# LayerNorm statistics of every ninth group on ScalarE, one conv chunk of two bands back on VectorE, and weights loaded and prepared later, in a fused attention and feed-forward block

## The chip, the cores and the metric

The kernel runs on one core of a Trainium2 chip. The metric is the device time of one execution in microseconds (us). The engines are named as in the profile: PE is TensorE's matmuls and PEld its weight loads, DVE is VectorE, ACT is ScalarE, POOL is GpSimd, and SP is the engine that here only issues transfers.

## The reference, cut to what matters

The input is 16 images of 128 channels by 96 x 96 pixels in float32. Each image goes through one transformer block:

```
xn1 = layernorm(x over channels)                    # per pixel, 9216 pixels per image
q, k, v = xn1 @ wq.T, xn1 @ wk.T, xn1 @ wv.T        # 8 heads of 16 channels
q, k = l2norm over the pixels                       # attention between channels
attn = softmax(q k^T / sqrt(16))                    # 16 x 16 per head
x = x + (attn v) @ wp.T
xn2 = layernorm(x over channels)
h1 = w_in @ xn2                                     # 1x1, 128 -> 512 channels
h2 = depthwise 3x3 convolution of h1                # one 3x3 filter per channel
x = x + w_out @ gelu(h2)                            # 1x1, 512 -> 128
```

The LayerNorm needs, for each pixel, the mean and the variance over the 128 channels and the power -1/2 of the variance.

## The kernel before, in words

**Tiling.** Channels lie on the 128 partitions. An image has 8 bands of 12 rows (1152 pixels), 24 units of 4 rows (384 pixels) and, for the LayerNorms, 18 groups of 4 x 128 pixels. The 512 hidden channels are 4 chunks of 128.

**One LayerNorm group** (`pixels`; suffix a for the first norm, b for the second). PE transposes four 128 x 128 tiles into one PSUM bank `pT` (`forth`, L609), so that pixels lie on partitions. DVE takes mean and sum of squared deviations with `bn_stats`, two tiles per instruction (`stats`, L616), into `st`. POOL makes the variance (`variance`, L623) and its power (`power`, L627) into `rstd`. For norm b DVE makes the shift `nb` (L631). ACT writes the scaled tiles to `zT` (`scaled`, L663 for a, L667 for b). For norm a PE adds each tile to a Gram matrix (`gram`, L677), from which the attention follows as small matrices per image. PE transposes back (`back`, L714), and ACT copies to the padded tile `xn` (`place`, L718, L720, L724). There are two `pT` banks for both norms. In image 0 the groups of norm a and the first five of norm b use the four `h` banks, and DVE scales half of each (L650, L654). The attention's result is one matrix per image, applied by `mix` (L566), with the residual added by ACT and a transfer (L575, L578), or by DVE in image 0 (L572).

**Feed-forward, by band and chunk** (`conv_job`). PE makes the hidden chunk (`hidden`, L899) and ACT copies it to `h1` (`kept`, L904, and the two halo rows, L895). Of the nine taps of the depthwise filter, ACT multiplies two or three (`product`, L912), and POOL-issued transfers add them up (`add_products`, L921). DVE does the remaining six or five with one fused multiply-add over 1152 pixels each (`tap`, L917). ACT applies GELU (L925). The fourth chunk is done in some bands by PE alone (`by_matmuls`, L967): nine matmuls per unit, with the 1x1 and the tap multiplied together beforehand in `comp`, and GELU straight from PSUM (L973). Which bands these are is said by `by_pe`:

```python
def by_pe(g):
    k = NG - 1 - g
    return k in PE_LAST if k < NB else k % PE_OF in PE_BANDS
```

`ffn_out` (L990) multiplies the four chunks by `w_out`, DVE adds the result to `x` (L997), and SP stores the band (L1001).

**The order.** Every piece of work is an `op` of a class `Plan`, with an engine, a place, an estimated cost and the tiles that it reads and writes. `Plan.order()` runs a list scheduler over them at build time: an engine takes its ready operation of the lowest place. A place is the position in the sequence of conv jobs plus an offset per kind from the table `AT`. So each engine has a fixed list of instructions, which it works off in order, and waits stand where the list and the data put them. The times in `Plan` are estimates for ordering only.

**The start.** SP loads the bands of `x` (L546). ACT issues the loads of the small vectors, of `wv` and of the depthwise weights `dw` (L276, L283, L288), and, after its third `place` copy, five loads of the other weights (L420 to L424). DVE first prepares `unit` and `ratio` from `dw` (L487 to L493) and the shift vectors (L478 to L482), and only then takes its first `bn_stats`.

Of the kernel before, what the change touches and what calls it, by code (L numbers as in the profile page):

```python
# [9 lines left out]
F32 = mybir.dt.float32  # L10
AF = mybir.ActivationFunctionType
ALU = mybir.AluOpType
# [5 lines left out]
UR = 4  # L18
BR = 12
PE_CHUNK = 3  # L20
PE_BANDS = (0,)
PE_OF = 2
PE_LAST = (0, 1, 2, 4, 5, 7)
TINY = 1e-20
UNIT_MIN = 1e-18
# [5 lines left out]
X1_BUFS, XB_BUFS, PR_BUFS, H3_BUFS, ZT_BUFS = 2, 6, 5, 10, 3  # L31
IN_TURN = ("tr", "h3", "pr", "xb", "x1")
AT = dict(
    load_w=20.7, weights=-42.35, zeros=-138.3, load_a=-151.9, forth_a=0.1, stats_a=-36.15, variance_a=263.5,
    power_a=249.55, scaled_a=74.15, gram=2.55, back_a=-28.75, place_a=112.3, attention=-146.85, mix=-33.95,
    residual=283.8, mixed=-159.7, add_x=-437.65, forth_b=0.35, stats_b=-221.75, variance_b=76.3, power_b=-236.6,
    shift_b=-162.65, scaled_b=19.7, back_b=1.45, place_b=-30.7,
    halo=161.95, hidden=3.15, kept=-18.75, products=83.25, add_last=-139.85, tap=10.15,
    add_first=-120.05, gelu=196.55, conv=2.95, conv_gelu=9.4, out=6.5, add=-10, store=164.8, mix_0=-40.75,
    residual_0=378.9, mixed_0=-198.6, add_x_0=-364.75, gram_0=9.85, forth_a_0=-6.55, forth_b_0=2.65,  # L40
    stats_a_0=-99.05, stats_b_0=-205.9, scaled_a_0=-81.4, scaled_b_0=247.4, back_a_0=-172.15, back_b_0=-50.5,
    place_a_0=-98.9, place_b_0=-35, shift_b_0=-201.25, late=-145.5,
)
STEP = dict(scaled=0.3, hidden=0.1, products=0.5, tap=0.166, conv=1.6, conv_tap=0.03, out=0.8, out_part=0.05)
SLACK = 300
NORM1_END = 6.0
EARLY = 5
WAIT = dict(POOL=350, SP=1300, ACT=1300)
T_WEIGHTS = 12000
T_VARIANCE = 420  # L50
T_POWER = 1000
T_ADD, T_MOVE = 3060, 1640
# [2 lines left out]
class Plan:  # L55
# [14 lines left out]
    def op(self, engine, ns, place, work, reads, writes, result, own=None, dma=0, two=False):  # L70

        k = len(self.ops)
        needs = {}
        for t in reads:
            if t in self.writer:
                needs[self.writer[t]] = True  # L80
        for t in writes:
            if t in self.writer:
                needs[self.writer[t]] = True
            for r in self.readers.get(t, ()):
                needs[r] = True
# [12 lines left out]
        self.ops.append((engine, ns, place, work, list(needs), new, result, own or result, dma, two))  # L98
# [111 lines left out]
def tile_restormer_block(  # L210
# [76 lines left out]
    per_unit = const.tile([P, NCH], F32, name="per_unit")  # L287
    nc.scalar.dma_start(out=dw, in_=w_dw.rearrange("(n p) o kh kw -> p n (o kh kw)", p=P))  # L288

    wvb = const.tile([P, 1], F32, name="wvb")  # L290
    ccol = const.tile([P, 2, 2], F32, name="ccol")
    ncq = const.tile([1, P], F32, name="ncq")
    none = const.tile([P, 1], F32, name="none")
# [56 lines left out]
    def at(kind, place, i=1):  # L350
        return place + AT[kind if i else kind + "_0"]
# [25 lines left out]
    def dve(ns, p, f, r, w, two=False):  # L377
        op("DVE", ns, p, f, r, w, ns + 120 + SLACK, ns + 120, two=two)
# [1 line left out]
    def add(p, f, r, w):  # L380
        op("POOL", 950, p, f, r, w, 1400 + SLACK, dma=T_ADD)

    def move(p, f, r, w, ns):
        op("SP", 60, p, f, r, w, 900 + SLACK, dma=ns)

    def act(ns, p, f, r, w):
        op("ACT", ns, p, f, r, w, ns + 150 + SLACK, ns + 150)
# [20 lines left out]
    def weights(p):  # L408
# [4 lines left out]
        def loads():  # L413
            a, b = (h3p.tile([P, BR * W], F32, tag="h3", name=f"weights_{k}") for k in range(2))
            v["win"] = a[:, :HID].rearrange("p (n c) -> p n c", c=P)
            v["wout"], v["wp"] = a[:, HID : 2 * HID], a[:, 2 * HID : 2 * HID + P]
            v["wqk"], v["wqkT"] = b[:, : 2 * P], b[:, 2 * P : 4 * P]
            v["wt"] = b[:, 4 * P : 8 * P].rearrange("p (t c) -> p t c", c=P)
            v["centre"], v["w1centre"], v["wvT"] = b[:, 8 * P : 9 * P], b[:, :P], b[:, P : 2 * P]
            nc.scalar.dma_start(out=v["wqk"][:, :P], in_=wq)  # L420
            nc.scalar.dma_start(out=v["wqk"][:, P:], in_=wk)
            nc.scalar.dma_start(out=v["wp"], in_=wp)
            nc.scalar.dma_start(out=v["win"], in_=w_in.rearrange("(n p) c kh kw -> p n (c kh kw)", p=P))
            nc.scalar.dma_start(out=v["wout"], in_=w_out.rearrange("c j kh kw -> c (j kh kw)"))  # L424

        def transposed(kind, parts, kept, gives):

# [68 lines left out]
            for n in range(NCH):  # L496
                nc.vector.tensor_scalar(v["wt"][:, n, :], v["win"][:, n, :], unit[:, n : n + 1], None, ALU.mult)

        op("ACT", 400, at("load_w", p), loads, [], mine, T_WEIGHTS, dma=2 * T_MOVE)
        dve(1400, at("weights", p), units, [], [("w", "in")])  # L500
        dve(400, at("weights", p), shifts, [], [("w", "in"), ("w", "conv"), ("w", "shift")])
        transposed(
            "weights", lambda: [v["wqk"][:, :P], v["wqk"][:, P:], v["wp"], wv_sb], keep_qkp, ["qk"]
        )
# [35 lines left out]
    def load(p, i, b):  # L540
        key = x_key(i, b, False)

        def go():
            pool, of = (xpool, xbs) if key == "xb" else (x1pool, x1s)
            of[i, b] = pool.tile([P, BR * W], F32, tag="x", name=f"x_{i}_{b}")
            nc.sync.dma_start(out=of[i, b], in_=x_band(i, b))  # L546

        move(p, go, [], [(key, (i, b), s) for s in range(UPB)], T_MOVE)

    def norm(i, second, place_of):  # L550

# [40 lines left out]
        def pixels(s, m):  # L592
# [18 lines left out]
            def stats(j):  # L611
# [5 lines left out]
                    d["st"][:, j, :], d["pT", qs[h]][:, k : k + 2, :].rearrange("p t c -> p c t")  # L617
                )

            def variance():  # L620
                d["mv"] = d["st"].rearrange("p j (t v) -> p (j t) v", v=3)
# [6 lines left out]

            def shift():
                nb = d["nb"] = small.tile([P, QB * QT], F32, tag="nb", name=f"nb_{name}_{m}")  # L630
                nc.vector.scalar_tensor_tensor(nb, d["mv"][:, :, 1], -1.0, d["rstd"], ALU.mult, ALU.mult)  # L631

            def zT(q):
                if q in zTs:
# [71 lines left out]
        def channels(s, u):  # L706

            d = {}

            def back():  # L710
                d["pB"] = p_bk.tile([P, UT], F32, tag="bk", name=f"pB_{name}_{u}")
                for j in range(TPU):
                    q, k = divmod(u * TPU + j, QT)
                    nc.tensor.transpose(d["pB"][:, j * P : (j + 1) * P], zTs[q][:, k, :P], ident)  # L714

            def place():
                if second:
                    nc.scalar.activation(interior(i, u), rows(d["pB"]), AF.Identity, bias=b2)  # L718
                else:
                    nc.scalar.copy(interior(i, u), rows(d["pB"]))  # L720

            def place_row(k, r, row):
                to = window(xns[k], r, 1, 1)
                nc.scalar.activation(to, rows(d["pB"])[:, row : row + 1, :], AF.Identity, bias=b2)  # L724

            copies = []
            if second and u % UPP == 0 and u > 0:
                copies.append((part_of(i, u * UR - 1)[0], PART + 1, 0, UPP))
            if second and u % UPP == UPP - 1 and u < NU - 1:
# [5 lines left out]
            act(t_act(UT, 1) - 43 if second else t_copy(UT), at("place" + ab, s, i), place, [pb, ("w", "shift")], [z_unit(i, u)])  # L735
# [340 lines left out]
```

## Time and profile before

| what | value |
|---|---|
| median of 3 runs | 4175.92 us (4175.73 to 4176.47) |
| the profiled execution | 4175.62 us |
| its span in the profile | 4173.9 us |
| busy: PE, PEld, DVE, ACT, POOL | 4142.5, 2679.6, 4070.0, 3693.7, 2479.5 us |
| transfers | 827.64 MB, mean 198 GB/s |

The profile covers one execution from its first to its last instruction, the span. The execution took 1.7 us more than that. A group of instructions is given by line, engine and operation, with the tile written, the tiles read, the count, the busy time, the mean duration of one, and the idle time of the engine just before. Successive instructions of one engine overlap, so the distance from start to start is less than a duration. Where a mean is used as a cost, this matters.

### The profile page before, as it was taken

What the parts mean: (1) busy time and instruction counts of PE and PEld (TensorE: products, weight loads), DVE (VectorE), ACT (ScalarE), POOL (GpSimd) and SP (SyncE); (2) the same over time, 40 slices, a digit from 0 to 9 for tenths busy, and PEclk for the clock granted to TensorE, in tenths of its full rate; (3) what the DMA queues carried; (4) which work ended last, traced back from release to release, by engine and by line L of the source; (5) the groups of instructions that cost most, each with busy time, mean ns of one, the idle gap of its engine ahead of it and who ended that gap; (6) DMA issues with size and microseconds to landing.
All of it is one profiled execution on the core that took longest, in us unless ns stands there. A gap on an engine that the chain in (4) does not pass through costs nothing.

```text
span 4173.9 us, 52446 instructions
## 1 busy us (share of the span) xinstructions
PE 4142.5 (99%) x17457; PEld 2679.6 (64%) x17457; DVE 4070.0 (98%) x4676; ACT 3693.7 (88%) x6970; POOL 2479.5 (59%) x2391
## 2 busy tenths in 40 slices
PE   8999999999999999999999999999999999999999
PEld 7666666666666666666666666666666666666565
DVE  6999999999999999999999999999999999999998
ACT  5899989899899989989898898998998999899885
POOL 4656566565665656656576565666756567565442
PEclk9999999999999999999999999999999999999999
DMA  2999999999999999999999998999999999998997
GB/s 88 197 188 215 194 208 208 203 208 197 205 208 201 204 198 212 200 205 211 193 202 205 199 215 185 211 200 209 208 198 202 201 209 201 203 204 184 201 193 159
DMA packets 203935, 827.64 MB, mean 198 GB/s; under 512 B 23568, under 2 KB 24976, under 8 KB 203664
## 3 DMA queue, kind: packets, MB, share of 16 engines
q0 software_dynamic: 164160, 672.47, 83.0%
q1 hardware_dynamic: 37152, 151.01, 9.9%
q8 instruction: 138, 2.26, 0.2%
q10 hardware_dynamic: 2352, 0.81, 0.1%
q14 instruction: 133, 1.09, 0.1%
HBM read 148.26 MB, written 75.50 MB: 54 GB/s over the span
## 4 chain that ended last, share of the span: by engine, by line
PE 88%; DVE 4%; DMA 3%; ACT 3%; POOL 1%; issue 1%; ACTq 0%; POOLq 0%; DVEq 0%
PE h L967 25%; PE h L990 21%; PE h L899 19%; PE g L677 5%; PE h L566 5%; DVE h L917 3%; PE pB_b L714 3%; PE pT_b L609 3%; PE pB_a L714 3%; PE pT_a L609 2%; DMA h<-pr 2%; DMA pr<-pr 1%; ACT pr L912 1%; ACT h L904 0%; DVE st_a L616 0%
## 5 line engine op out<-in xcount | busy, mean ns | idle before, releaser
L917 DVE SCALAR_TENSOR_TENSOR h<-h,ratio,h 128x1152 f32<-128x1152 f32 x2104 | 2915.2, 1407 | 3.6
L912 ACT ACTIVATE pr<-h,ratio 128x1152 f32<-128x1152 f32 x1018 | 1301.6, 1290 | 65.1 <-DMA h<-pr 37.6
L967 PE MATMUL h<-xn,comp 128*128 128x384 f32 x3564 | 1269.3, 485 | 0.0
L990 PE MATMUL h<-h,woutT 128*128 128x384 f32 x3072 | 1137.1, 486 | 1.0 <-ACT h L904 0.4
L899 PE MATMUL h<-xn,winT 128*128 128x384 f32 (+1 forms) x2676 | 1078.6, 500 | 1.1 <-ACT h L904 1.0
L967 PEld LDWEIGHTS h<-xn,comp 128*128 128x128 f32 x3564 | 647.9, 189 | 394.9 <-issue 12.6
L921 POOL DMA_DIRECT2D pr<-pr x573 | 562.6, 989 | 493.2 <-ACT pr L912 385.7
L904 ACT COPY h<-h 128x384 f32<-128x384 f32 (+1 forms) x1338 | 667.9, 520 | 182.0 <-PE h L899 162.1
L990 PEld LDWEIGHTS h<-h,woutT 128*128 128x128 f32 x3072 | 554.2, 190 | 327.2 <-issue 10.3
L921 POOL DMA_DIRECT2D h<-pr x445 | 424.7, 956 | 531.5 <-DVE h L917 119.0
L899 PEld LDWEIGHTS h<-xn,winT 128*128 128x128 f32 x2676 | 475.5, 190 | 269.2 <-issue 39.2
L917 DVE SCALAR_TENSOR_TENSOR h<-h,ratio 128x1152 f32<-128x1152 f32 x446 | 627.3, 1411 | 13.5 <-ACT h L904 5.3
L925 ACT ACTIVATE h<-h 128x1152 f32<-128x1152 f32 x448 | 536.0, 1198 | 17.0 <-DMA h<-pr 13.9
L627 POOL TENSOR_TENSOR rstd_a<-ve_a,mhalf 128x4 f32<-128x4 f32 x288 | 534.4, 1856 | 12.7
L627 POOL TENSOR_TENSOR rstd_b<-ve_b,mhalf 128x4 f32<-128x4 f32 x288 | 506.8, 1760 | 11.3
L667 ACT ACTIVATE zT<-pT_b,nb_b,rstd_b 128x128 f32<-128x128 f32 x1132 | 430.5, 478 | 24.3 <-DVE nb_b L631 21.3
L623 POOL TENSOR_SCALAR ve_b<-st_b 128x4 f32<-128x4 f32 x288 | 293.8, 1020 | 219.8 <-DVE st_b L616 204.8
L623 POOL TENSOR_SCALAR ve_a<-st_a 128x4 f32<-128x4 f32 x288 | 276.8, 961 | 226.0 <-DVE st_a L616 211.8
L663 ACT ACTIVATE zT<-pT_a,rstd_a 128x128 f32<-128x128 f32 x1080 | 316.6, 406 | 19.8 <-POOL rstd_a L627 19.4
L677 PEld LDWEIGHTS g<-zT 128*128 128x128 f32 x2304 | 297.2, 191 | 56.9 <-issue 3.8
L677 PE MATMUL g<-zT 128*128 128x129 f32 x2304 | 305.2, 275 | 0.0
L566 PE MATMUL h<-xn,mwT 128*128 128x384 f32 x768 | 284.3, 490 | 5.6 <-ACT h L904 2.7
(173 smaller groups left out, 3578.6 us busy)
## 6 DMA issues: line engine op xcount, KB each, us to landing
pr<-pr POOLq DMA_DIRECT2D x573, 576.0 KB, 7.3
h<-pr POOLq DMA_DIRECT2D x445, 576.0 KB, 6.9
x<-in_x_dram SPq DMA_DIRECT2D x128, 576.0 KB, 6.2
out_dram<-x SPq DMA_DIRECT2D x127, 576.0 KB, 5.2
x<-in_x_dram POOLq DMA_DIRECT2D x122, 576.0 KB, 6.9
out_dram<-x SPq DMA_DIRECT2D x3, 192.0 KB, 1.9
weights<-in_L_conv_w_in_dram ACTq DMA_DIRECT2D x1, 256.0 KB, 2.9
weights<-in_L_conv_w_out_dram ACTq DMA_DIRECT2D x1, 256.0 KB, 3.0
```

What stands on the lines that cost most here:

```text
L566: nc.tensor.matmul(rows(pm), lhsT=mats[i][0], rhs=interior(i, u), start=True, stop=True)
L623: nc.gpsimd.tensor_scalar(ve, d["mv"][:, :, 2], 1.0 / C, EPS, ALU.mult, ALU.add)
L627: nc.gpsimd.tensor_tensor(rstd, d["ve"], mhalf, ALU.pow)
L677: nc.tensor.matmul(grams[i][:, : P + 1], lhsT=zt[:, :P], rhs=zt, start=(q == 0 and k == 0), stop=(q == NU * TPU // QT - 1 and k == QT - 1),)
L899: nc.tensor.matmul(rows(ph), lhsT=winT[:, n, :], rhs=window(xn, r0 + r, e - r, 1), start=True, stop=True)
L904: nc.scalar.copy(window(h1_, r, e - r, 1), rows(d.pop(("ph", r))))
L912: nc.scalar.activation(to, shifted(t), AF.Copy, scale=ratio[:, n, t : t + 1])
L917: nc.vector.scalar_tensor_tensor(h3, shifted(t), ratio[:, n, t : t + 1], onto, ALU.mult, ALU.add)
L921: nc.gpsimd.dma_start(out=to, in_=d["pr", t], accum_op=ALU.add)
L925: nc.scalar.activation(h3, h3, AF.Gelu)
L967: nc.tensor.matmul(d["pc"], lhsT=comp[:, t, :], rhs=window(xn, r0 + dy, UR, dx), start=(t == 0), stop=(t == 8),)
L990: nc.tensor.matmul(rows(d["po"]), lhsT=woutT[:, n, :], rhs=h3s[g, n][:, s * UR : (s + 1) * UR, :], start=(k == 0), stop=(k == NCH - 1),)
```

## The change

1. In every image one norm group in nine (group numbers 1 and 10 of norm a, 4 and 13 of norm b, not those that use the `h` banks) takes its statistics on ACT. For each of its four tiles one pass with `Identity` and scale -1/128 accumulates minus the mean, and one pass with `Square` and that value as bias accumulates the sum of squared deviations. The elementwise results go to a tile `junk` that nobody reads. The two `bn_stats` of the group on DVE are left out, and the sign in `shift` is turned.
2. `PE_BANDS` and `PE_OF` say 15 of 31 bands in place of 1 of 2. Counted over the 128 bands with the last 8 as they were, PE does the fourth chunk in 64 bands in place of 66, and DVE, ACT and the transfers in 64 in place of 62.
3. The five weight loads move from ACT's queue to SP's, behind the eight band loads of image 0. The preparation of `unit`, `ratio` and the shift vectors is ordered behind these loads, and in DVE's list it stands after the statistics of the twelfth group. ACT gets one small copy at its start, so that its table is loaded there.
4. The table `AT` has other values throughout, so all five lists are ordered anew.

```diff
-PE_BANDS = (0,)
-PE_OF = 2
+PE_BANDS = (0, 2, 4, 6, 8, 10, 12, 14, 16, 18, 20, 22, 24, 26, 28)
+PE_OF = 31
...
+BY_ACT_OF, BY_ACT_A, BY_ACT_B = 9, (1,), (4,)
+T_SQUARES = 840
...
-T_WEIGHTS = 12000
+T_START = 2300
...
+    none = const.tile([P, 1], F32, name="none")
+    nc.scalar.copy(none, ones)
...
+    junk = const.tile([P, P], F32, name="junk")
...
-            nc.scalar.dma_start(out=v["wqk"][:, :P], in_=wq)
...
+            nc.sync.dma_start(out=v["wqk"][:, :P], in_=wq)
...
-        op("ACT", 400, at("load_w", p), loads, [], mine, T_WEIGHTS, dma=2 * T_MOVE)
-        dve(1400, at("weights", p), units, [], [("w", "in")])
-        dve(400, at("weights", p), shifts, [], [("w", "in"), ("w", "conv"), ("w", "shift")])
+        op("SP", 60, at("load_w", p), loads, [], mine, 2500, dma=2 * T_MOVE)
+        dve(1400, at("weights", p), units, mine[:1], [("w", "in")])
+        dve(400, at("weights", p), shifts, mine[:1], [("w", "in"), ("w", "conv"), ("w", "shift")])
...
+            by_act = not early and m % BY_ACT_OF in (BY_ACT_B if second else BY_ACT_A)
...
+            def squares(k):
+                if k == 0:
+                    d["st"] = small.tile([P, QT, 3], F32, tag="st", name=f"st_{name}_{m}")
+                z, st = d["pT", qs[0]][:, k, :], d["st"]
+                nc.scalar.activation(junk, z, AF.Identity, scale=-1.0 / C, accum_out=st[:, k, 1:2])
+                nc.scalar.activation(junk, z, AF.Square, bias=st[:, k, 1:2], accum_out=st[:, k, 2:3])
...
-            for j in range(QB * QT // 2):
+            for k in range(QT if by_act else 0):
+                act(T_SQUARES, at("squares", s), lambda k=k: squares(k), [trs[0]], [bt])
+            for j in range(0 if by_act else QB * QT // 2):
                 dve(341, at("stats" + ab, s, i), lambda j=j: stats(j), [trs[2 * j // QT]], [bt])
```

Counted in the lists of instructions of the two built kernels, an instruction that is two passes in the profile counted once:

| engine | instruction | before | after |
|---|---|---|---|
| PE | `by_matmuls`, 128x384 | 1782 | 1728 |
| PE | `hidden`, 128x384 and 128x480 | 1118 and 220 | 1120 and 224 |
| DVE | `bn_stats` | 1152 | 1030 |
| DVE | `tap` | 2550 | 2562 |
| ACT | the new passes, `Identity` and `Square` | 0 | 244 and 244 |
| ACT | `product`; GELU 128x1152; GELU 128x384 | 1018; 445; 201 | 1022; 447; 195 |
| ACT | table loads | 32 | 32 |
| POOL | `add_products` | 1018 | 1022 |

Each of the new passes waits for the ACT instruction before it in the same group, since `junk` is written by all and the mean is read by the second of a pair.

More of the change, by code (lines that the diff above doesn't have):

```diff
@@ L33 @@
 AT = dict(
[L34 to L42, printed above, removed]
+    load_w=-34.85, weights=-6.45, zeros=-47.95, load_a=-161.5, forth_a=-10.95, squares=65.4, stats_a=-51.15,
+    variance_a=399.1, power_a=213.5, scaled_a=41.3, gram=2.65, back_a=-96.15, place_a=141.55, attention=-167.1,
+    mix=-61.8, residual=350, mixed=-113.3, add_x=-440.7, forth_b=-9.5, stats_b=-260.4, variance_b=84.1,
+    power_b=-188.25, shift_b=-165.65, scaled_b=42.65, back_b=-6.25, place_b=-60.25, halo=232.4, hidden=3.9,
+    kept=-66.15, products=36.15, add_last=-84.05, tap=3.85, add_first=-178.55, gelu=176.35, conv=3.8,
+    conv_gelu=3.25, out=8, add=-17.75, store=143.2, mix_0=-91.7, residual_0=543.2, mixed_0=-197.5,
+    add_x_0=-426.1, gram_0=52.5, forth_a_0=-185.6, forth_b_0=-10.2, stats_a_0=-136.45, stats_b_0=-206.45,
+    scaled_a_0=-6.15, scaled_b_0=303, back_a_0=-127.35, back_b_0=-75.15, place_a_0=-148.6, place_b_0=-120.85,
+    shift_b_0=-199.4, late=58.65,
 )
@@ L288, in tile_restormer_block @@
     nc.scalar.dma_start(out=dw, in_=w_dw.rearrange("(n p) o kh kw -> p n (o kh kw)", p=P))
+    none = const.tile([P, 1], F32, name="none")
+    nc.scalar.copy(none, ones)
     wvb = const.tile([P, 1], F32, name="wvb")
+    junk = const.tile([P, P], F32, name="junk")
     ccol = const.tile([P, 2, 2], F32, name="ccol")
     ncq = const.tile([1, P], F32, name="ncq")
-    none = const.tile([P, 1], F32, name="none")
     wqkT = const.tile([P, 2 * P], F32, name="wqkT")
@@ L381, in add, with move @@
         op("POOL", 950, p, f, r, w, 1400 + SLACK, dma=T_ADD)
-    def move(p, f, r, w, ns):
-        op("SP", 60, p, f, r, w, 900 + SLACK, dma=ns)
+    def move(p, f, r, w, ns, first=0):
+        op("SP", 60 + first, p, f, r, w, 900 + SLACK, dma=ns)
     def act(ns, p, f, r, w):
@@ L419, in loads @@
             v["centre"], v["w1centre"], v["wvT"] = b[:, 8 * P : 9 * P], b[:, :P], b[:, P : 2 * P]
-            nc.scalar.dma_start(out=v["wqk"][:, :P], in_=wq)
[L421 to L424, printed above, removed]
+            nc.sync.dma_start(out=v["wqk"][:, :P], in_=wq)
+            nc.sync.dma_start(out=v["wqk"][:, P:], in_=wk)
+            nc.sync.dma_start(out=v["wp"], in_=wp)
+            nc.sync.dma_start(out=v["win"], in_=w_in.rearrange("(n p) c kh kw -> p n (c kh kw)", p=P))
+            nc.sync.dma_start(out=v["wout"], in_=w_out.rearrange("c j kh kw -> c (j kh kw)"))
         def transposed(kind, parts, kept, gives):
@@ L546, in go @@
             nc.sync.dma_start(out=of[i, b], in_=x_band(i, b))
-        move(p, go, [], [(key, (i, b), s) for s in range(UPB)], T_MOVE)
+        move(p, go, [], [(key, (i, b), s) for s in range(UPB)], T_MOVE, 0 if i or b else T_START)
     def norm(i, second, place_of):
@@ L618, in stats @@
                 )
+            def squares(k):
[4 more added lines that the diff above has]
+                nc.scalar.activation(junk, z, AF.Square, bias=st[:, k, 1:2], accum_out=st[:, k, 2:3])
             def variance():
-                d["mv"] = d["st"].rearrange("p j (t v) -> p (j t) v", v=3)
+                d["mv"] = d["st"] if by_act else d["st"].rearrange("p j (t v) -> p (j t) v", v=3)
                 ve = d["ve"] = small.tile([P, QB * QT], F32, tag="ve", name=f"ve_{name}_{m}")
@@ L630, in shift @@
                 nb = d["nb"] = small.tile([P, QB * QT], F32, tag="nb", name=f"nb_{name}_{m}")
-                nc.vector.scalar_tensor_tensor(nb, d["mv"][:, :, 1], -1.0, d["rstd"], ALU.mult, ALU.mult)
+                nc.vector.scalar_tensor_tensor(
+                    nb, d["mv"][:, :, 1], 1.0 if by_act else -1.0, d["rstd"], ALU.mult, ALU.mult
+                )
             def zT(q):
@@ L734, in channels @@
             pe(110 * TPU, at("back" + ab, s, i), back, [(*zt_of(q), k) for q in quads for k in range(2)], [pb])
-            act(t_act(UT, 1) - 43 if second else t_copy(UT), at("place" + ab, s, i), place, [pb, ("w", "shift")], [z_unit(i, u)])
+            act(t_act(UT, 1) - 43 if second else t_copy(UT), at("place" + ab, s, i), place, [pb, ("w", "shift")] if second else [pb], [z_unit(i, u)])
             for k, r, row, of in copies:
```

## The prediction

> **What bounds the kernel now.** I read the page's busy shares first, then its chain of what ended last.
>
> ```profile
> PE 4142.5 (99%) x17457; PEld 2679.6 (64%) x17457; DVE 4070.0 (98%) x4676; ACT 3693.7 (88%) x6970; POOL 2479.5 (59%) x2391
> PE 88%; DVE 4%; DMA 3%; ACT 3%; POOL 1%; issue 1%; ACTq 0%; POOLq 0%; DVEq 0%
> ```
>
> PE and DVE are both nearly full, and 88% of the chain is PE's. A busy PE need not be at its peak, so I looked at the chain in order of time for PE's real pace, and at its start.
>
> ```profile
> 3.44 4.38 DMA dw<-in_L_conv_w_dw_dram
> 10.34 2.66 DVE st_a L616 x8
> 13.71 0.96 ACT L663
> 22.11 2.03 DMA weights<-in_L_conv_wk_dram
> ...
> 1793.46 5.81 PE h L967 x18
> 1799.28 1.94 PE h L899 x6
> ```
>
> Eighteen passes of 384 columns take 5.81 us, 0.323 us each, and the next line starts where this one ends. The page's mean of 485 ns for such a pass is a latency; 0.323 us is what it costs. At the start the chain runs through the depthwise weights, the table load (L663) and a weight load.
>
> Last, the busy time by stretches; the columns are length, PE, PEld, DVE, ACT, POOL, clock, DMA share and GB/s.
>
> ```profile
> 2400.00:2425.00 25.00, 25.00 (x111) 15.94 (x110) 24.79 (x31) 24.52 (x49) 17.53 (x18) 1.00 1.01 224
> 100.00:4100.00 4000.00, 3986.91 (x16685) 2568.01 (x16684) 3942.59 (x4429) 3609.07 (x6788) 2425.86 (x2259) 1.00 0.95 202
> ```
>
> From 100 to 4100 us PE is idle for 13 us, DVE for 57, ACT for 391; the transfers use 95%. PE sets the pace, DVE is 1% behind it, and ACT has 9.8% left. PE is idle for another 15 us before 100 us and for 4 at the end.
>
> **PE, part 2 of the change.** 54 matmuls leave `by_matmuls`, two passes each: 108 x 0.323 = -34.9 us. Two chunks come back to `hidden`: 4 passes of 384 and 8 of 480 columns, 4 x 0.323 + 8 x 0.40 = +4.5 us (0.40 is 0.323 scaled by the width). Sum: **-30.4 us**, on the engine that carries the chain.
>
> **DVE.** 122 `bn_stats` go and 12 taps come. The timeline gives their distance from start to start.
>
> ```profile
> 2009.44 0.43 DVE L616 BATCH_NORM_STATS2 st_b<-pT_b 128x6 f32<-128x256 f32 x1
> 2009.78 0.54 DVE L997 TENSOR_TENSOR x<-h,x 128x384 f32<-128x384 f32 x1
> ```
>
> So 122 x 0.34 = -41.5 us; three taps in a row cost about 1.33 us each, 12 x 1.33 = +16.0 us. Sum: -25.5 us. DVE has 44 us more idle time than PE in the middle; with 5 us less relief it stays behind PE, and I book nothing for it.
>
> One rule speaks otherwise. "Perfetto Trace Analysis", section Identifying the Most-Contended Engine, judges TensorE's headroom by the weight loads' busy share and not by matmul time. By that, PE's 64% would leave a third free and DVE would be the bound. The sum would then hold -25.5 in place of -30.4. The gapless 0.323 us above decides for PE here.
>
> **ACT.** 244 pairs of passes come. No row shows an accumulating pass, so I bound a pair by these groups.
>
> ```profile
> L663 ACT ACTIVATE zT<-pT_a,rstd_a 128x128 f32<-128x128 f32 x1080 | 316.6, 406 | 19.8 <-POOL rstd_a L627 19.4
> L780 ACT COPY gs<-g 128x129 f32<-128x129 f32 x16 | 4.8, 298 | 0.7 <-PE g L677 0.6
> L873 ACT COPY d<-g 128x1 f32<-128x1 f32 x15 | 2.8, 187 | 0.0
> ```
>
> `Identity` with a constant scale is like L780, 0.298 us. `Square` with a per-partition bias is like L663, median 0.387. The passes wait for each other, so they don't overlap. A waiting pass starts 0.03 us after the end of the one before: L904 at 2013.32 for 0.48, the `product` that reads it at 2013.83. That gives 0.298 + 0.387 + 0.06 = 0.75 us as the lower end. If the accumulator costs a small instruction like L873 and a wait each time, the pair costs 0.75 + 2 x 0.217 = 1.18 us. The list shows no such instruction, so I take 0.85, near the lower end. 244 x 0.85 = +207 us, between 183 and 288. Two more chunks of products, copies and GELU add 4 x 1.16 + 2.5 = +7 us. Table loads stay 32, so nothing comes for a function missing from the table.
>
> "ScalarE: Activation LUTs", section What ACT_TABLE_LOAD costs, gives 186 ns plus 0.833 ns per element, and about 93 ns per pointer operand. An estimate from that is 293 + 386 ns a pair, 166 us for all. The section Rules for kernel authors in the same page sends multiplies and adds to VectorE. By it the change is a loss, as two tiles cost DVE 0.34 us and ACT 1.7; whether it counts depends on who has time.
>
> ACT then has 3609 + 214 = 3823 us of work in the middle, which lasts about 3970 us: 96.3%. Its cover shrinks from 391 to about 145 us. Queued behind the passes are `kept` (PE's next `hidden` and DVE's taps wait for it), `place` and `scaled` (PE's transposes), `product` (the transfers) and GELU (`ffn_out`). The group's `pT` bank is held longer too: DVE needs 0.76 us for its two `bn_stats`, ACT 4 x 0.85 with other work put between the pairs. I charge 10 us of new PE stalls: 61 groups at 0.16 us. The ends are 0 (every wait hidden, as in the 25 us stretch above, where ACT was busy 98.1% and PE never idle) and 50 us (0.8 us a group). Less than 0 is possible only up to the 13 us that PE idles now, if DVE's relief removes them.
>
> **The start.** DVE's first `bn_stats` could start when PE's first transposes are done, at about 6.2 us instead of 10.3: -4.1. The table load (13.71 to 15.0) leaves the chain: -1.3. ACT's wait for the weight load at 22.11: -2.0. Together -7.4 us. The preparation itself, DVE from 7.85 to 10.26, now stands at a point where DVE keeps pace with PE with little to spare: +2.4. Sum: **-5.0 us**, between -7.4 and 0. The weight loads pass SP's eight band loads and no store. They are first needed at 42.7 us, while the transfers are idle from 27 to 38, so I book nothing; if late, they cost a wait of 3 us, about what such a load takes to land.
>
> **Transfers.** Four more `add_products`, about 3 us of all 16 engines each by share and count (95% of 4000 us over some 1250 transfers): 12 us on 95%. Hidden as long as 3% stay free; POOL (59%) covers their issue.
>
> **The sum.** Span 4173.9 - 30.4 - 5.0 + 10 = 4148.5; plus the 1.7 us outside the span, **4150 us**. The profiled execution (4175.62) lies 0.3 us under the median, so the same number stands for the median. About 0.2% (8 us) is what a measurement of this kernel can tell from no change: faster is below 4167.6, slower above 4184.3.
>
> **Rivals.** *The pass holds up PE and the gain is eaten.* The longer hold of `pT` or a late `kept` reaches PE with 0.5 us in each of the 61 changed groups: 30 us, about 4170. For it: only two `pT` banks, and POOL and ACT behind them. Against it: of all PE's waits in before, those for `pT` come to 2.3 us.
>
> *ACT becomes the bound: slower.* An engine with a fixed list and many partners can't be busy all the time. With c for the highest share that ACT can hold in the middle, that stretch lasts 3823 / c, and the rest about 170.6 us with the time outside the span. It decides from c below 95.25%, where the total passes 4184 us. At 95% it is 4195, at 94% 4238. A pair at 1.18 us does the same already at c = 97%: 3904 / 0.97 + 170.6 = 4195. For it: no stretch of 100 us shows ACT above 94%. Against it: DVE, with as many partners, holds 98.6%, and ACT itself held 98.1% for 25 us.
>
> *DVE is the bound after all:* -25.5 in place of -30.4, so 4155. This is within the forecast.
>
> *The change doesn't do what it says:* the counts of the lists exclude that it moves another number of bands or loads tables. What is left is that the new order is worse or better in itself; its effect lies in the stalls.
>
> **Chances and range.** Forecast (with the DVE case) 0.68, own range 4138 to 4167. Gain eaten 0.13. ACT bound 0.19. The range of 8 in 10 goes from 4128 (all of the start, and the 13 us of idle time gone) to 4195 (ACT's share at 95%). Faster 0.68, same 0.13, slower 0.19.
>
> **What would show it.** Right: PE busy near 4112 us with 13 to 25 us idle from 100 to 4100; the pair near 0.85 us; ACT near 96% in the middle; first `bn_stats` near 6.2 us. Wrong: a pair over 1.2 us, PE's waits led by ACT's copies or by `pT`, DVE's idle time doubled, or transfers waiting with their share at 98%.

## The result and the profile after

The changed kernel took 4181.5 us (median of 22 runs, 4173.61 to 4187.42) against 4174.81 for the kernel before in the same session (22 runs, 4169.46 to 4178.29). The ratio is 1.0017, 95% interval 1.0011 to 1.0023: slower by 7 us. The profiled execution (4185.59 us) lies 4 us over its median, so the two traces differ by 10 us where the medians differ by 7.

The busy shares and the stretch from 100 to 4100 us (columns as before):

```profile
PE 4128.2 (99%) x17361; PEld 2664.1 (64%) x17361; DVE 4056.1 (97%) x4566; ACT 3840.4 (92%) x7953; POOL 2444.3 (58%) x2395
```

```profile
100.00:4100.00 4000.00, 3960.82 (x16558) 2546.29 (x16557) 3916.37 (x4312) 3744.96 (x7747) 2385.25 (x2260) 1.00 0.95 202
```

PE's busy time fell by 14.3 us, and its idle time in the long stretch rose from 13 to 39. DVE's idle time rose from 57 to 84. ACT stands at 93.6%, not 96, and its idle time fell from 391 to 255 us, not to 145. So PE and DVE have less work and wait more: their work went down and the time didn't. (The chain of what ended last can't be followed back beyond the last 12% of this trace, so it doesn't answer to the 88% of before.)

What PE waits for (engine and line that wait, what releases it: total, times, longest):

```profile
PE h L1007 <- ACT h L921: 10.2, 7, 4.3
PE h L615 <- DMA x<-in_x_dram: 5.5, 1, 5.5
PE pB_a L731 <- ACT zT L678: 5.5, 4, 3.3
PE h L571 <- ACT h L921: 5.4, 4, 3.0
PE pB_a L731 <- ACT xn L737: 3.5, 5, 1.9
```

The second line is the load of the first band, there in both kernels; the others are ACT's `kept`, `scaled` and `place`. The first and the fourth are these in before:

```profile
PE h L990 <- ACT h L904: 0.4, 1, 0.4
PE h L566 <- ACT h L904: 2.7, 4, 1.0
```

PE's waits of 0.3 us and more after 100 us come to 10.6 us before and 36.2 after. A wait has a second price. PE's timeline, and then stretches with the granted clock third from the end:

```profile
252.40 7.12 PE L571 MATMUL h<-xn,mwT 128*128 128x384 f32 x12 [3.05 <-ACT h L921]
```

```profile
252.00:254.00 2.00, 1.60 (x3) 0.99 (x4) 2.00 (x3) 2.00 (x4) 1.07 (x2) 0.50 1.09 217
254.00:259.00 5.00, 5.00 (x10) 2.60 (x9) 5.00 (x6) 4.50 (x12) 4.17 (x4) 0.55 1.03 206
260.00:265.00 5.00, 5.00 (x16) 2.83 (x15) 5.00 (x4) 5.00 (x8) 1.73 (x2) 1.00 1.01 174
```

After 3.05 us of waiting the clock is halved for some 6 us, and twelve passes take 7.12 us, 0.59 each instead of 0.323. Added up over the span in steps of 20 us, the clock that was not granted is 3.6 us before and 15.4 after. So the trace adds up: idle time 31.4 to 55.7 us (+24), clock 12 us, less PE's booked 30: +6 of the 10. The remaining 4 us lie within PE's busy time, as delays too short to be listed. They show when PE is measured from start to start. With every kind of pass at its median distance in before, PE's passes need 4117 us before and 4087 after, 30 less. What PE takes beyond that, halved clock and short delays included, is 47 us before and 87 after. So 30 us of work went and 40 us of delay came.

The clock's part differs from execution to execution. The profiled one has the lowest mean clock of the 22, 0.996; the others have 0.996 to 0.999, and the one at 0.999 is the fastest (4173.61 us). So 12 us is at the upper end.

Why was ACT late at 252.40? ACT's timeline just before:

```profile
249.52 1.28 ACT L942 ACT_TABLE_LOAD   x1
250.82 1.16 ACT L942 ACTIVATE h<-h 128x1152 f32<-128x1152 f32 x1
251.89 0.84 ACT L921 COPY h<-h 128x384 f32<-128x384 f32 x2
```

`kept` stands in ACT's list behind a table load and a GELU. No accumulating pass is near. Another big wait, at 2594.10, has another origin. POOL, DVE and PE around it:

```profile
2584.66 5.90 POOL L636 TENSOR_SCALAR ve_a<-st_a 128x4 f32<-128x4 f32 x1
2591.11 2.53 POOL L640 TENSOR_TENSOR rstd_a<-ve_a,mhalf 128x4 f32<-128x4 f32 x1
```

```profile
2582.45 8.05 DVE L934 SCALAR_TENSOR_TENSOR h<-h,ratio,h 128x1152 f32<-128x1152 f32 x6
```

```profile
2594.10 0.73 PE L731 MATMUL pB_a<-ident,zT 128*128 128x128 f32 x2 [3.33 <-ACT zT L678]
```

`variance` handles 128x4 numbers, and the same instruction takes 0.2 us where no tap runs. Here it takes 5.90 and ends as DVE's six taps end. The power, ACT's `scaled` and PE follow. Five such instructions of 4.7 to 5.9 us are in this trace, all in groups with ACT statistics; the longest in before took 3.1.

### The profile page after: what moved, and what is told of

It is laid out like the page before. It is cut to its first block, busy times and chain, and to the rows that moved or that the text cites. A ratio compares the mean times of both kernels' runs of the same rounds, so it can differ in the third digit from the quotient of the medians.

```text
span 4183.9 us, 53131 instructions
## 1 busy us (share of the span) xinstructions
PE 4128.2 (99%) x17361; PEld 2664.1 (64%) x17361; DVE 4056.1 (97%) x4566; ACT 3840.4 (92%) x7953; POOL 2444.3 (58%) x2395
## 5 line engine op out<-in xcount | busy, mean ns | idle before, releaser
L929 ACT ACTIVATE pr<-h,ratio 128x1152 f32<-128x1152 f32 x1022 | 1311.4, 1293 | 68.1 <-DMA h<-pr 41.9
L984 PE MATMUL h<-xn,comp 128*128 128x384 f32 x3456 | 1241.9, 487 | 0.7 <-ACT h L921 0.7
L916 PE MATMUL h<-xn,winT 128*128 128x384 f32 (+1 forms) x2688 | 1063.7, 500 | 3.2 <-ACT h L921 1.1
L984 PEld LDWEIGHTS h<-xn,comp 128*128 128x128 f32 x3456 | 628.3, 190 | 382.8 <-issue 11.7
L938 POOL DMA_DIRECT2D pr<-pr x575 | 546.5, 958 | 555.3 <-ACT pr L929 338.7
L942 ACT ACTIVATE h<-h 128x1152 f32<-128x1152 f32 (+1 forms) x450 | 537.9, 1201 | 13.4 <-DMA h<-pr 13.2
L640 POOL TENSOR_TENSOR rstd_a<-ve_a,mhalf 128x4 f32<-128x4 f32 x288 | 499.1, 1734 | 13.0 <-POOL ve_a L636 0.2
L640 POOL TENSOR_TENSOR rstd_b<-ve_b,mhalf 128x4 f32<-128x4 f32 x288 | 496.1, 1728 | 12.2
L682 ACT ACTIVATE zT<-pT_b,nb_b,rstd_b 128x128 f32<-128x128 f32 x1132 | 433.7, 496 | 10.6 <-DVE nb_b L644 9.0
L636 POOL TENSOR_SCALAR ve_a<-st_a 128x4 f32<-128x4 f32 x288 | 309.8, 1076 | 200.0 <-DVE st_a L622 167.8
L636 POOL TENSOR_SCALAR ve_b<-st_b 128x4 f32<-128x4 f32 x288 | 264.7, 927 | 239.7 <-DVE st_b L622 210.9
```

Source lines behind the costliest of these rows:

```text
L640: nc.gpsimd.tensor_tensor(rstd, d["ve"], mhalf, ALU.pow)
L682: nc.scalar.activation(zT(q)[:, k, :P], d["pT", q][:, k, :], AF.Identity, bias=d["nb"][:, t : t + 1], scale=d["rstd"][:, t : t + 1],)
L916: nc.tensor.matmul(rows(ph), lhsT=winT[:, n, :], rhs=window(xn, r0 + r, e - r, 1), start=True, stop=True)
L929: nc.scalar.activation(to, shifted(t), AF.Copy, scale=ratio[:, n, t : t + 1])
L938: nc.gpsimd.dma_start(out=to, in_=d["pr", t], accum_op=ALU.add)
L942: nc.scalar.activation(h3, h3, AF.Gelu)
```

## The experiments

Three theories stood at the start. A: ACT's added passes make ACT late for PE. B: the new order of the lists makes the waits, whatever the work. C: the variance of the groups on ACT comes late because POOL is held up while DVE runs taps. "Kept order" below means that every engine's list stands as in the named kernel. The kernel before differed by some us between sessions, so all ratios are to its runs in the same session; "us" is the ratio applied to 4175. PE idle is from 100 to 4100 us (13.1 before, 39.2 after). The runs whose names begin with a change the kernel after, all others the kernel before.

| run | ratio (95%) | us | PE idle |
|---|---|---|---|
| a1_stats_back | 1.0033 (1.0022 to 1.0045) | +14 | 41.9 |
| a2_both | 1.0129 (1.0115 to 1.0142) | +54 | 62.4 |
| a4_neither | 1.0045 (1.0032 to 1.0059) | +19 | 50.5 |
| a3_ve_on_act | 1.0002 (0.9993 to 1.0011) | +1 | 30.6 |
| b1_start | 1.0002 (0.9993 to 1.0011) | +1 | 10.8 |
| b2_bands | 1.0097 (1.0084 to 1.0110) | +41 | 62.5 |
| b3_squares | 1.0066 (1.0053 to 1.0080) | +28 | 36.5 |
| d2_table_alone | 1.0034 (1.0021 to 1.0047) | +14 | 19.5 |
| c1_old_table | 1.0119 (1.0100 to 1.0138) | +50 | 73.3 |
| p1_pe_less | 0.9974 (0.9963 to 0.9984) | -11 | 22.8 |
| p2_dve_less | 1.0017 (1.0008 to 1.0026) | +7 | 15.2 |
| p3_both_less | 0.9977 (0.9968 to 0.9987) | -10 | 28.8 |
| p4_act_less | 0.9990 (0.9981 to 0.9999) | -4 | 14.6 |
| p5_pe_act_less | 0.9954 (0.9942 to 0.9967) | -19 | 23.0 |
| p6_pe_dma_less | 0.9955 (0.9942 to 0.9967) | -19 | 20.4 |
| a7_dma_less | 0.9999 (0.9990 to 1.0008) | 0 | 33.7 |
| g1_kept_order | 1.0338 (1.0324 to 1.0352) | +141 | 101.4 |
| g2_kept_ve | 1.0372 (1.0358 to 1.0386) | +155 | 110.8 |

**The statistics, in the kept order of after.** a1: `squares` emits the group's two `bn_stats`, no passes.

```diff
             def squares(k):
-                nc.scalar.activation(junk, z, AF.Identity, ...)
-                nc.scalar.activation(junk, z, AF.Square, ...)
+                if k % 2 == 0:
+                    stats(k // 2)
```

> The changed kernel with every engine's list kept as it is, but in the groups with statistics on ScalarE the two passes per tile are replaced by DVE's bn_stats (one for each two tiles, at the same point of the order). ACT loses about 193 us of work (244 pairs of 0.79 us), DVE gains 122 x 0.34 = 41 us. Theory A (ACT's added work is what makes ACT late for PE, and after the longest of these waits PE's clock halves): PE's idle time from 100 to 4100 us falls from 39 to below 20 us and the mean granted clock returns to 0.999; the time falls by 10 to 30 us, to 4152 to 4172. Theory B (the new order of the lists makes the waits, not ACT's work): PE's idle time stays above 30 us, the clock below 0.998, the time within 8 us of the changed kernel or longer. Theory C (the variance of these groups comes late, because POOL is shut out while DVE runs taps): as theory A, but only the waits that follow a long ve go, 10 to 15 us.

a2 keeps the passes as well, with their results unused.

> As the changed kernel, every list kept; in the groups with statistics on ScalarE the passes stay on ACT but nobody uses their result, and DVE takes the statistics with bn_stats at the same point of the order. So ACT's added work stays and only what waits for it is changed; DVE has 41 us more. Theory A: PE's idle time from 100 to 4100 stays above 30 us and the clock below 0.998; the time is 4175 to 4200. Theory C: no ve over 4 us is left, PE's idle time falls by 10 us or more, and the time is 4160 to 4175. Theory B: as A.

a1 is 0.16% slower than after (0.03 to 0.29 by the two intervals), and its waits stand where after's do:

```profile
PE h L1004 <- ACT h L918: 9.8, 7, 3.5
PE h L571 <- ACT h L918: 5.3, 4, 3.1
PE pB_a L728 <- ACT xn L734: 3.4, 3, 2.0
```

They come to 37.6 us in all; the 4.3 us wait at 141.7 is still 3.5, the one of 3.05 us is there, only the one at 2594 is gone. So A falls as the cause of the waits, and exchanging the statistics is a gain of some 7 us in this order (1 to 12). The mean clock of a1's profiled execution is back at 0.999, as A had it, but that is the fastest of its six; the others have 0.996 to 0.998. With both pieces of work (a2) it is 54 us over before, beyond both of its ranges: 193 us more on ACT without DVE's relief cost 40 us. a4 is the fourth corner, with neither.

```diff
             def squares(k):
-                ...
+                d["st"] = fixed
```

> The changed kernel, all lists in their order, with neither passes nor bn_stats in the 61 groups (their statistics are a constant tile): against after it lacks 193 us of passes on ACT, against a1_stats_back 41 us of bn_stats on DVE. If passes and bn_stats each cost what a2_both shows (42 and 48 us): some 4135 to 4150. If each costs only when the other is there too, as DVE's relief brought nothing in p2_dve_less: 4170 to 4185, like after and a1_stats_back, and what is left is the new order's.

It was slower than after, with less work on ACT and DVE. Neither of the two readings expected that. Its trace has `variance` held up for longer still:

```profile
715.35 10.58 POOL L634 TENSOR_SCALAR ve_a<-st_a 128x4 f32<-128x4 f32 x1
```

PE's `back` waits 2.98 us behind this one. But it belongs to a group that still has its `bn_stats`: seven of a4's `variance` instructions take over 4 us, and three of them, the two longest included, are of such groups. Taps run here without a break from 715.15 to 725.87 us, and the variance ends with them. So C isn't a matter of the groups on ACT alone.

The corners do not add up (+19, +7, +14, +54), so the passes have no price of their own. In a3 ACT makes `ve` for its groups:

```diff
+                if k == QT - 1:
+                    nc.scalar.activation(ve, st[:, :, 2], AF.Copy, bias=EPS, scale=1.0 / C)
...
+                if by_act:
+                    return
                 nc.gpsimd.tensor_scalar(ve, ...)
```

> As the changed kernel, but in the groups with statistics on ScalarE the variance ve (128x4) is made by ACT right after the last pass, and POOL makes only the power. ACT gets 61 instructions of about 0.2 us, POOL loses 61 ve. Theory C: the waits of PE of 4.3, 3.3 and about 1 us after 141, 2594 and 3354 us go with their halved clock; the time falls by 8 to 15 us, to 4166 to 4174. Theory A and B: the power on POOL still waits for DVE's taps, the other PE waits stay, and the time moves by less than 6 us, 4176 to 4186.

It brought 0.15% (6 us, 2 to 11): theory C holds for about that much. The rest of the long spans moved to `power` (four of 3.8 to 5.9 us). It is level with the kernel before, and no complete version was faster than it.

**One part at a time, replanned.** b1 is the kernel before with part 3, b2 with part 2, b3 with part 1, each with before's own table (b3 with `squares=65.4` besides); d2 is the kernel before with the new table and its old places for the weights; c1 has all parts with the old table.

```diff
+# b2:
-PE_BANDS = (0,)
-PE_OF = 2
+PE_BANDS = (0, 2, 4, ..., 28)
+PE_OF = 31
+# d2:
-    load_w=20.7, weights=-42.35, zeros=-138.3, load_a=-151.9, forth_a=0.1, stats_a=-36.15, ...
+    load_w=20.7, weights=-42.35, zeros=-47.95, load_a=-161.5, forth_a=-10.95, stats_a=-51.15, ...
```

> The kernel before with the start of the changed kernel alone: weight loads on SP's queue behind the eight band loads, the depthwise weights prepared later, one copy at ACT's start that loads its table; the table's places load_w and weights are those of the changed kernel. Nothing else changes. In the changed kernel's profile the first tap stands 6.0 us earlier (89.3 against 95.3). If PE's work afterwards is as in before, the time falls by 4 to 7 us, to 4168 to 4171. If the lead is lost in later waits, it is 4173 to 4180.

> The kernel before with the new band rule alone (PE_BANDS, PE_OF): 54 matmuls of two passes fewer on PE (-30.4 us net), 12 taps more on DVE (+16), 7 us more on ACT; statistics, start and table as before. If PE sets the pace, as the prediction has it, 4144 to 4150. If PE and DVE set it together (DVE's relief of 41 us was worth 48 us in the pair of runs after and a2_both), PE's relief is paid for by DVE's taps: 4175 to 4195, with PE's idle time from 100 to 4100 us grown by about what its work shrank, 13 to some 40 us.

> The kernel before with the statistics of every ninth group on ACT alone (squares=65.4 in its own table; bands, start and all other places as before): DVE -41 us, ACT +193 us, PE the same. If DVE's relief is worth nothing and ACT's passes cost PE a few stalls, as the prediction has it, 4178 to 4190. If relief and passes nearly cancel whatever the order (+42 for the passes, -48 for the relief), 4165 to 4175. If the passes themselves hold PE up (theory A), over 4190. PE's own work of 4140 us forbids less than about 4160.

> The kernel before with the values of the new table alone (the two places of the weight loads and their preparation kept): all work the same, the order new. Theory B (the new order itself makes the waits): 4185 to 4200, PE's waits of 0.3 us and more grow from 10 to over 30 us. If the order costs nothing and the parts do: 4172 to 4180, waits near 10 us.

> All three parts of the change (statistics, bands, start) with the table of the kernel before: work as in after, the order by the old values. Theory B: the waits go and the parts bring what they save on PE, 4150 to 4165. If the parts make the waits whatever the table (A and C, and DVE kept on the path by its taps): 4178 to 4195, with 30 us or more of PE's waits.

b1: the first `bn_stats` starts at 6.71 us instead of 10.26, but the first `hidden` at 93.25 instead of 91.95, and the first band is done at the same time. The lead is lost before any band. d2: the same work under the new table costs 14 us by itself. That is the time which B expected, but not the waits: those of 0.3 us and more after 100 us grow from 10.6 to 16.1 us, not to over 30. Its trace gives 11.6 us, nearly all of it idle time (31.4 to 41.8 us). Of these 10 us 4 lie before 100 us; PE waits 6.5 us there until 15.8 us, where before has waits of 4.2 and 1.3 us and after one of 2.4. d2 keeps before's start, and after has another, so what the order costs in after itself isn't measured. The rest of after's waits comes with the other parts, as d2 and a1 side by side show (100 to 4100 us, d2 first):

```profile
100.00:4100.00 4000.00, 3980.54 (x16676) 2569.80 (x16675) 3936.24 (x4424) 3601.43 (x6791) 2387.30 (x2259) 1.00 0.95 201
100.00:4100.00 4000.00, 3958.12 (x16550) 2537.93 (x16548) 3947.18 (x4431) 3597.38 (x6779) 2389.00 (x2259) 1.00 0.95 202
```

a1 has the new table, the bands and the start, but no pass on ACT. From start to start its PE passes need 30 us less than d2's and have 27 us more of delay (86 against 59), and the two take the same time (both +14 us, the difference uncertain by 7). So under the new table nearly all that PE saves comes back as delay.

c1 was the opposite of what B expected: with the old order the same parts cost 50 us, 43 more than with the new one, so that offsets which fit one amount of work don't fit another. Bands or statistics alone cost 41 and 28; b2 and c1 lie above both of their ranges, and b3 (4205 us) in the one set for theory A, which a1 speaks against. That b2 and b3 measure mainly such a misfit, and not the price of the parts, is argued from c1 and not shown.

**Relief in the kept order of before.** Now the order stays the same, though it was fitted to before's work; no run has p1 with a table of its own. p1 leaves out one of nine matmuls in 49 units, p2 the `bn_stats` of the 61 groups, p4 makes the four `scaled` of a norm a group one instruction, which shortens ACT's work (by 104 us in the long stretch); p3 is p1 with p2, p5 is p1 with p4, p6 is p1 with fewer rows in the transfers, and a7 has those in the kernel after.

```diff
+# p1:
+            if t == 4 and (g // 2 * UPB + s) % 4 == 0:
+                return
+# p2:
+                if by_act:
+                    d["st"] = fixed
+                    return
+# p4:
+                if not second and not early:
+                    nc.scalar.activation(zT(q)[:, :, :P], d["pT", q], AF.Copy, scale=d["rstd"][:, :1])
+                    return
+# p6, a7:
+            if t != DMA_TAPS[0]:
+                nc.gpsimd.dma_start(out=to[:, : BR - 2, :], in_=d["pr", t][:, : BR - 2, :], accum_op=ALU.add)
```

> The kernel before, all lists in their order, with the middle one of the nine matmuls left out in 49 of the 198 units of by_matmuls (that part of the convolution is left out): PE 98 passes of 0.323 us less, -31.7 us, everything else as before. If PE alone sets the pace, as the prediction has it, the time falls by the same: 4143 to 4150. If DVE (57 us idle) and ACT bind beside it, PE only waits longer: 4155 to 4172, with PE's idle time from 100 to 4100 us up from 13 to 25 us or more.

> The kernel before, all lists in their order, with the two bn_stats left out in the 61 groups that the change moves to ACT (their statistics are a constant tile; nothing comes in their place): DVE -41 us, everything else as before. By the prediction, which books DVE's relief at nothing: 4172 to 4177. If DVE binds beside PE, as the 48 us between a2_both and after suggest: 4150 to 4168.

> The kernel before, all lists in their order, with p1's 49 matmuls and p2's 122 bn_stats both left out (PE -31.7 us, DVE -41 us). If DVE is what holds back PE's relief in p1_pe_less (4159.8, 0.9974 of before), the rest of it arrives now: 4140 to 4150. If ACT or the coupling of all holds it back: 4155 to 4168, like p1_pe_less or a little above, as p2_dve_less was 7 us above before.

> The kernel before, all lists in their order, with the four scaled instructions of each norm a group outside image 0 made as one instruction of 512 columns with the first tile's factor (the factors of the other three tiles are left out): some 0.5 us less on ACT in each of 270 groups, about -130 us, everything else as before. If ACT's lateness is no part of the time of before: 4170 to 4177. If ACT's time counts although it is idle for 391 us: 4150 to 4168.

> The kernel before, all lists in their order, with p1's 49 matmuls left out and p4's relief of ACT (PE -31.7 us, ACT about -130 us). If ACT is what holds back PE's relief in p1_pe_less: 4138 to 4148, PE's waits back near 10 us. If DVE holds it back: 4153 to 4163, as p1_pe_less.

> The kernel before, all lists in their order, with p1's 49 matmuls left out and 573 of the 1018 add_products (those from one product tile to another) moving 10 of their 12 rows (the sums of the other two rows are left out): PE -31.7 us, the transfers 55 of 828 MB less, their share from 95% to about 89%. If the transfers hold back PE's relief in p1_pe_less (0.9974 of before): 4138 to 4148, ratio about 0.993, and the share of 89% brings ACT's waits for transfers (46 us or more in p1) down by half. If ACT and the order alone hold it back: 4153 to 4162, as p1_pe_less.

> The changed kernel, all lists in their order, with the same 573 (here 575) add_products moving 10 of their 12 rows: the transfers 55 of 830 MB less, everything else as after. If the transfers' lateness is what the changed kernel's longer PE waits come from: 4150 to 4168. If those waits come from where kept, scaled and GELU stand in ACT's new list: 4176 to 4186.

p1 is the run that decides. PE has 31.7 us less to do, and 11 arrive (6.7 to 15.4), about a third. Its long stretch:

```profile
100.00:4100.00 4000.00, 3977.16 (x16630) 2554.95 (x16629) 3951.43 (x4441) 3613.95 (x6800) 2449.92 (x2262) 1.00 0.95 202
```

PE's idle time here grows from 13 to 23 us, and over the whole span its busy time falls by 23 instead of 32. From start to start PE's passes need 31 us less and have 18 us more of delay (65 against 47). DVE isn't what holds PE back: p3 equals p1, and p2 alone, with 41 us less on DVE, is 7 us slower than before. With ACT or the transfers relieved as well, 19 us arrive, 8 more than in p1 (uncertain by 7). That ACT or the transfers hold PE's relief back isn't shown by this. ACT relieved alone gives 4 us (p4, 0 to 8), so 4 of p5's 8 us are no more than that; the transfers relieved alone weren't run in before, and in after they bring 7 (a7). By the ranges set beforehand, p4, p5 and p6 (4171, 4156 and 4156 us by their ratios) all lie in the one that speaks against this. In p6 the transfers' share is 0.90, and ACT's waits for them fall from 97 us in p1 to 48:

```profile
ACT pr L912 <- DMA h<-pr: 51.1, 55, 3.2
ACT pr L912 <- DMA pr<-pr: 31.6, 41, 2.9
ACT h L925 <- DMA h<-pr: 14.0, 10, 4.7
```

```profile
ACT pr L912 <- DMA h<-pr: 28.7, 34, 3.3
ACT pr L912 <- DMA pr<-pr: 10.0, 12, 2.7
ACT h L928 <- DMA h<-pr: 9.4, 8, 3.9
```

The first three lines are p1's, the others p6's. The same relief of the transfers brought the changed kernel 7 us (a7, 0.9999 against 1.0017), between its two expectations. In the profiled executions its PE waits fall from 36.2 to 29.9 us and the clock loss from 15.4 to 7.0; the waits of after at 141.7, 252.4 and 2594.1 are still there, in the same size. The other 12 us of the relief, which are missing in p5 and p6 too, are not found.

**The passes in the kept order of before.** g1 emits them where the `bn_stats` stood, and g2 adds a3's edit.

```diff
             def stats(j):
+                if by_act:
+                    squares(2 * j)
+                    squares(2 * j + 1)
+                    return
```

> The kernel before, all lists in their order, with the passes on ACT put exactly where the bn_stats of the 61 groups stood: DVE -41 us, ACT +193 us, no replanning. If the new order is what costs (b3_squares, the same work replanned with the old offsets, took 4205), the time is 4165 to 4178 here. If the passes cost by themselves whatever the order: 4190 to 4210.

> As g1_kept_order, and the variance of these 61 groups is made by ACT behind its last pass and not by POOL, which waits while DVE runs taps (theory C). Theory C: 5 us less than g1_kept_order or more, as a3 was 6 us under after. If POOL's lateness is covered here: the same as g1_kept_order within 3 us, or 5 us more for 61 instructions of 0.2 us on ACT.

Both missed by far: 141 and 155 us. PE's waits of 0.3 us and more come to 96 us, led by 22 waits of norm b's `back` for `place`, 32.9 us. So 61 blocks of some 3 us, put into an ACT list that wasn't planned for them, cost much more than in after, and the replanning that after has is needed. a3's edit, a gain in after, is a loss here.

## Why the prediction was wrong

**PE's relief, -30.4, booked in full: this step failed.** The gapless 0.323 us per pass was right, and so was the count. PE's passes need 30 us less. But that PE is busy 99% of the time doesn't make PE the only bound. With before's order kept, p1 gives about a third: 11 us (7 to 15) of 31.7. Under the new table 27 of 30 us come back as delay (a1 against d2). PE's waits come mostly from ACT, in both kernels, but which engine would have to be relieved for the rest to arrive stays open: p4, p5 and p6 don't settle it.

**The new order: the second failure.** I named it among the rivals and gave it no price. d2 measures it at 14 us (9 to 20) for equal work, with the start of before. Put into the sum, p1's 11 and these 14 turn -25 into about +8, near the +7 measured, but that is luck: the sum still holds the start's 5 us and the passes' 10 us, which weren't found, and not the 7 us gained between a1 and after. With these put right the sum gives -4. The 11 us between that and the +7 measured are about p1's 11, which don't arrive under the new table.

**The stalls, 10 us.** The trace has 26 us more of waits and 12 us of halved clock; the clock was not in the sum at all. That the passes would make the stalls is shown false by a1, which has the same waits without a single pass. The page "TensorE: Matmul & The Clock Gate", section What's actually happening, has the clock halved by default and again after an idle window of about 3.4 us. Here 3.05 us were enough, and so was a wait of 1.86 at 3035.5 us (the clock is 0.59 from 3037 to 3041), while one of 2.14 at 3262.8 left it at 1.00. Nor does the length alone decide: waits of 3.06 us in a1 (at 249.6) and of 3.33 in a7 (at 2587.3) left it at 1.00, and after one of 2.13 in a1 (at 3261.4) it is 0.66 from 3261 to 3266.

**The start, -5.0: gone** (b1). The lead existed, and was lost in image 0 before the first `hidden`. In after the first `hidden` comes 6.1 us earlier and the first band is still done at the same time (156.9 us against 157.1).

**ACT.** The pair was sized well from start to start, by a wrong reason: 0.79 us for 0.85 forecast, 193 us for 207. ACT's busy time grew by less, 147 us in place of 214 (3693.7 to 3840.4; a1, without the passes, has 3693.4), so that ACT kept more room than forecast. The instruction that I had left out since the list doesn't show it is there, but its span overlaps the next pass (start, duration):

```profile
211.42 0.31 ACT L630 ACTIVATE junk<-pT_b 128x128 f32<-128x128 f32 x1
211.59 0.23 ACT L630 ACTIVATION_READ_ACCUMULATOR junk<-pT_b 128x1 f32 x1
211.85 0.37 ACT L631 ACTIVATE junk<-pT_b,st_b 128x128 f32<-128x128 f32 x1
212.12 0.19 ACT L631 ACTIVATION_READ_ACCUMULATOR junk<-pT_b,st_b 128x1 f32 x1
212.21 0.47 ACT L737 COPY xn<-pB_a 128x384 f32<-128x384 f32 x1
```

**DVE's relief at nothing** is borne out alone (p2, even +7). But exchanged against the passes it brings the 7 us between a1 and after, and next to the passes its loss costs 47 (a2 against after), so relief of DVE and load on ACT have no separate prices. **The transfers, hidden at 95%,** were not wholly: 55 MB less bring 7 or 8 us (a7; p6 against p1). But the change adds only 2.4 MB, in proportion 0.3 us, so nothing was about right for this term.

**The rivals.** "Gain eaten" named the right outcome and the wrong place: it put the loss into the 61 groups. Of the signs of being wrong, PE's waits are led by ACT's copies, as was said; the pair and the first `bn_stats` (6.67 us) were nearly as forecast all the same. ACT as the bound is excluded by a1, which is slower than after with ACT at 88%. Run after run, order (+14, d2), bands and start (0, a1 against d2) and statistics (-7, after against a1) lead to the +7; each step is uncertain by 5 to 8 us, and that they end there is by construction. How much of the bands' 0 is due to their 12 taps, 7 us on ACT and 12 us of transfers isn't shown.

The low end of the range, 4128, is 3 us above what its terms give (4150 - 10 - 2.4 - 13 = 4125); nothing hangs on it.

## What to carry to other kernels

Where several engines stand above 90%, the busiest one's saved time need not arrive in full; leave out a little of its work with the order kept, and see which part arrives before booking the change (here a third, and almost nothing under the new table, so a third was itself too much). A rewritten order table is a change of its own: run it alone on the old work, and expect single edits under a table that was fitted to other work to mislead (here +28 to +50 us). Look for what a late small instruction holds up before moving a large one: 61 instructions on 128x4 numbers moved from POOL to ACT were worth about as much (6 us, 2 to 11) as the exchange of 41 us on DVE for 193 us on ACT (7 us, 1 to 12).

## What the runs showed of the chip

- An accumulating ScalarE pass is followed by an ACTIVATION_READ_ACCUMULATOR of 128x1, 193 ns after `Square` and 222 after `Identity`; a dependent pair takes 0.79 us from start to start.
- A GpSimd instruction on 128x4 numbers took up to 5.9 us (10.6 in a4) beside runs of taps, 0.2 without. "SBUF — State Buffer", section Who interferes with whom, says that a VectorE instruction with two SBUF inputs contends with a GpSimd instruction that reads SBUF; the taps read two SBUF tiles, and the row agrees. The row at 2584.66 us shows it held up until the sixth tap in a row was over.
- Taking work away can cost time: p2 (41 us less on DVE) and a4 (passes and `bn_stats` both gone) are slower than the kernels that they are made from. In p2 the transfers of POOL's queue take 84.4% of the span for the same bytes, 83.0% before; what makes them slower isn't settled.
